# Two graph-attention layers on one core: layer 2's table in degree order, own rows by a plain DMA, another share for TensorE, another seam

## The chip, the cores and the metric

The kernel runs on one core of one Trainium2 chip. The metric is the device time of one execution in microseconds; lower is better. The kernel before takes 5581.57 us, the median of three runs (5579.89 to 5582.52).

## The reference

There are 10000 nodes of 768 features and 170000 edges, sorted by destination (each node has one edge to itself in the list; the layer adds another). All is in fp32. A graph-attention layer projects every node, gives every edge a softmax weight over the edges that end in the same node, and sums the projected source rows with these weights:

```
def gat_conv(x, edge_index, W, a_src, a_dst, bias, heads, out_ch, concat):
    ...
    xl = (x @ W).reshape(n, heads, out_ch)
    alpha_src = jnp.einsum('nhc,hc->nh', xl, a_src)
    alpha_dst = jnp.einsum('nhc,hc->nh', xl, a_dst)
    e = jax.nn.leaky_relu(alpha_src[src] + alpha_dst[dst], 0.2)
    ...                                   # softmax of e over the edges of one dst
    out = jax.ops.segment_sum(xl[src] * alpha[:, :, None], dst, num_segments=n)
    return out + bias

h = gat_conv(x, edge_index, W1, a_src1, a_dst1, b1, 4, 256, True)
h = relu(layer_norm(h, g1, be1)) + (x @ Wr1 + br1)
h1 = h
h = gat_conv(h, edge_index, W2, a_src2, a_dst2, b2, 1, 768, False)
h = layer_norm(h, g2, be2) + (h1 @ Wr2 + br2)
return _layernorm(x + h)
```

## The kernel before

The work has three stages. PE is TensorE, DVE is VectorE, ACT is ScalarE, POOL is GpSimd and SP is SyncE, which only issues DMAs.

**Stage A, the table of layer 1 and the order.** For each of 79 tiles of 128 nodes PE computes x @ W1 (L166, called from L633), ACT and DVE the two attention numbers of every head (L638, L641), and SP stores 128 rows of 1032 floats (4128 B: 1024 features, 4 source and 4 destination numbers) to `table1` (L645). SP also loads x, two tiles ahead (`load_x`, L590). Between the tiles a generator, `prepare` (L185 to L410), does one step at a time of sorting the nodes by their number of in-edges, many first. It computes each node's place in that order (`rank`, L321), scatters node numbers and edge positions to four lists in DRAM (L305), loads these back with SP (`order_d`, L336; 10112 pieces of 16 bytes each), and makes `slots`: for every tile of 128 nodes of nearly equal degree a list of source nodes, one column per slot. Column 0 of a tile is the node itself. A missing edge points to a row of its own at the table's end that weighs nothing. A second generator, `weight_steps`, loads the weights of layer 2 (`w2`) and of layer 1's residual (`wr1`).

**Layer 1** (`ordered_layer1`, L656) goes over the 79 sorted tiles in the order `TURNS`: from few slots (8) up to many (41 in the middle) and down again to 9. The sum over the tiles is 1377 slots. A ring of 28 slots in SBUF (`RING1`) holds gathered rows; `Ring.fetch` issues one indirect DMA on POOL for each slot (`gather`, L413), 128 rows of 4128 B, as soon as the slot's old rows were used. For a tile of n slots `weights_of` takes the softmax weights of all n (`logits`, `normalised`; it needs all n rows) and lets PE sum the first `on_pe(t)` slots (at most `ON_PE1`): ACT makes diagonal matrices of weights (L691) and PE multiplies them with the rows into `acc` (L697). DVE adds the other slots to `acc`: one of `SHARE` = 4 directly with the weight (L496, four instructions), the other three as plain sums (L492) of rows that ACT has multiplied (L485). The weights of the next tile are taken three slots (`LEAD`) before the end of a tile. Then DVE normalises the tile (L538 to L554), adds the residual product x @ Wr1 (L755), PE transposes (L560) and multiplies with W2 (L166, `to_layer2`), SP stores the transposed h1 (L767), ACT copies the product to a row of 770 floats (L716), and POOL scatters this row to `table2` at the nodes' own numbers (`store`, L718), a tile and a half later. POOL also gathers x for the residual (`fetch_x`).

**Layer 2** (`ordered_layer2`, L804) takes the same tiles in the same order with rows of 770 floats (3080 B), one head and a ring of 38 slots (`RING2`). PE sums columns 512 to 767 of every slot (L850, L851), DVE columns 0 to 511 (L496). `residual` computes x + h1 @ Wr2 on PE (L862, L865) from `fetch_x`: h1 loaded by SP (L826), x gathered by POOL. `norms` makes the two layer norms, and POOL scatters the finished rows to the output (L884). At the seam between the layers the first 8 gathers are issued first, then Wr2 is loaded into the space of W2, small vectors are loaded by ACT's queue, and `product(brT, wr2)` gives the constant br1 @ Wr2.

The order within each engine's queue is written out by hand (`manual_schedule`); a queue runs in its order, and waits are on semaphores. The tile of 41 slots does not fit a ring and takes another path (`attend_parts`); no weights are taken ahead for it or for a tile with too many slots after it.

Of the kernel before, what the change touches and what calls it, by code (L numbers as in the profile page):

```python
# [28 lines left out]
F32 = mybir.dt.float32  # L29
# [5 lines left out]
P = 128  # L35
# [10 lines left out]
RING1 = 28  # L46
# [4 lines left out]
SHARE = 4  # L51
ON_PE1 = 5

# [25 lines left out]
def gnn_kernel(ctx, tc, x, x_cols, src, dst, src_col, dst_col, W1, a_src1, a_dst1, b1, g1, be1, Wr1, br1,  # L79
# [5 lines left out]
    C1, C2 = H1 * DH1, H2 * DH2  # L85
    R1, R2 = C1 + 2 * H1, C2 + 2 * H2
    NT = -(-N // P)
# [43 lines left out]
    fits = consts.tile([1, 1], I32, name="fits")  # L131
    lift = consts.tile([P, 1], F32, name="lift")

    def spread(pool, v, name):
# [3 lines left out]
        nc.scalar.dma_start(b, bass.AP(tensor=v.tensor, offset=v.offset, ap=[[0, P], [1, n]]))  # L138
        return b
# [45 lines left out]
    def prepare():  # L185

        with tc.tile_pool(name="prep", bufs=1, side="right") as pool, \
# [146 lines left out]
            with nc.allow_non_contiguous_dma(reason="16 bytes a node"):  # L334
                for to, d in zip([sorted_] + others, order_d):
                    nc.sync.dma_start(to, d.rearrange("(t p) f -> p t f", p=P))  # L336
                    yield
            for other in others:
                nc.vector.tensor_add(sorted_, sorted_, other)
# [89 lines left out]
    class Ring:  # L429


        def __init__(self, pool, table, row, size):
            self.table, self.size, self.issued = table, size, 0
            self.rows = pool.tile([P, size, row], F32, name="ring")

        def fetch(self, upto):
            for q in range(self.issued, min(upto, TOTAL)):
                gather(self.slot(q), self.table[:, :], slots[:, q:q + 1])
                self.issued = q + 1
# [12 lines left out]
    def logits(small, ring, lo, hi, ad, heads, c, top=None):  # L452


        n = hi - lo
        e = small.tile([P, ring.size, heads], F32, name="e")[:, :n]
        for a, b, rows in ring.parts(lo, hi):
            nc.vector.tensor_tensor(e[:, a - lo:b - lo], rows[:, :, c:c + heads],
                                    ad[:, None, :].to_broadcast([P, b - a, heads]), op=OP.add)
# [110 lines left out]
    def spread_br1(pool, name):  # L570

        b = pool.tile([P, K1], F32, name="br1_c")
        with nc.allow_non_contiguous_dma(reason="1024 numbers"):
            nc.scalar.dma_start(b, br1.rearrange("(k p) -> p k", p=P))
        to = pool.tile([P, K1, P], F32, name=name)
        nc.vector.tensor_copy(to, b[:, :, None].to_broadcast([P, K1, P]))
        return to
# [4 lines left out]
    with tc.tile_pool(name="w1", bufs=1) as w1p, tc.tile_pool(name="l1", bufs=2) as io, \  # L582
# [15 lines left out]
        nc.vector.memset(none[:, :C1], 0.0)  # L598
        nc.vector.memset(none[:, C1:], -BIG)
        nc.scalar.dma_start(table1[NP:NP + 1, :], none)  # L600
        nc.scalar.dma_start(table2[NP:NP + 1, :], none[:, C1 - C2:C1 + 2 * H2])
# [5 lines left out]
        def weight_steps():  # L607

            brT = spread_br1(w1p, "brT")
            yield
            yield
            load(w2, W2)
            for i, a in enumerate((a_src2, a_dst2)):
# [16 lines left out]
        for t in range(NT):  # L632
# [23 lines left out]
    def ordered_layer1():  # L656
        nonlocal ps_big
        with tc.tile_pool(name="b1", bufs=1) as pool, tc.tile_pool(name="small1", bufs=2) as small, \
                tc.tile_pool(name="ps_acc1", bufs=2, space=PSUM) as ps_acc, \
                tc.tile_pool(name="ps_h1", bufs=1, space=PSUM) as ps_big, \  # L660
                tc.tile_pool(name="ps_r1", bufs=1, space=PSUM) as ps_r, tc.manual_schedule():
            ring = Ring(pool, table1, R1, RING1)
            ring.fetch(SLOTS[0])
# [10 lines left out]
            def on_pe(t):  # L674


                return min(max((2 * SLOTS[t] - 15) // 5, 1), ON_PE1, SLOTS[t])

            def weights_of(t):

                n, m = SLOTS[t], on_pe(t)
                e, _ = logits(small, ring, FIRST[t], FIRST[t] + n, ring.slot(FIRST[t])[:, C1 + H1:], H1, C1)
                yield e
# [28 lines left out]
            def store(t):  # L712

                nonlocal full
                row = pool.tile([P, R2], F32, name="row")
                nc.scalar.copy(row, full[:, :R2])  # L716
                full = None
                nc.gpsimd.indirect_dma_start(  # L718
                    out=table2[:, :], out_offset=bass.IndirectOffsetOnAxis(ap=nodes(t), axis=0),
                    in_=row, in_offset=None)  # L720

            for t in range(NT + 1):
# [54 lines left out]
                if live and not whole:  # L777
                    due(n)
                    acc = ps_acc.tile([P, 2 * BANK], F32, name="acc")
                    ad = small.tile([P, H1], F32, name="ad")  # L780
                    nc.vector.tensor_copy(ad, ring.slot(FIRST[t])[:, C1 + H1:])
                    attend_parts(small, ring, acc, acc, ad, None, H1, DH1, t)
# [21 lines left out]
    def ordered_layer2():  # L804
        nonlocal ps_big
        with tc.tile_pool(name="b2", bufs=1) as pool, tc.tile_pool(name="small2", bufs=2) as small, \
                tc.tile_pool(name="ps_acc2", bufs=2, space=PSUM) as ps_acc, \
                tc.tile_pool(name="ps_q2", bufs=3, space=PSUM) as ps_big, tc.manual_schedule():
            ring = Ring(pool, table2, R2, RING2)
            ring.fetch(SLOTS[0])  # L810

            wr2, parts = w2[:, :, :C2], [wr1[:, k, :] for k in range(K0)]
            load(wr2, Wr2)
            b2_b, g2_b, be2_b = (spread(pool, v, n) for v, n in ((b2, "b2"), (g2, "g2"), (be2, "be2")))
            more = pool.tile([P, C2], F32, name="out")
            nc.scalar.dma_start(more, bass.AP(tensor=br2.tensor, offset=br2.offset, ap=[[0, P], [1, C2]]))
            nc.vector.tensor_add(be2_b, be2_b, more)
            brT = spread_br1(pool, "brT")
            more = pool.tile([P, C2], F32, name="out")
            nc.scalar.dma_start(more, shift.to_broadcast([P, C2]))  # L820
            nc.vector.tensor_add(b2_b, b2_b, more)

# [114 lines left out]
    def general_path():  # L937
# [82 lines left out]
        def attend_chunks(keep, work, small, lists, table, row, heads, dh, t):  # L1020
# [10 lines left out]
            adm = keep.tile([P, 2 * heads], F32, name="adm")  # L1031
            nc.vector.tensor_copy(adm[:, :heads], acc[:, c + heads:])
            tmp = small.tile([P, heads], F32, name="tmp")
# [172 lines left out]
```

## Time and profile before

| | |
|---|---|
| median of 3 runs | 5581.57 us |
| profiled execution, its own time | 5586.68 us |
| span of its records | 5584.8 us |
| granted TensorE clock, mean | 0.939 |
| busy PE / DVE / ACT / POOL | 4822.9 / 4279.6 / 3140.8 / 3367.2 us |
| moved by DMA | 1581 MB, mean 283 GB/s |
| gathers of rows (L413) | 2754, 954 ns each |
| scatters of layer 2's rows (L718) | 79, 1079 ns each |
| stage A, layer 1, layer 2 | about 0 to 890, 890 to 3530, 3540 to 5585 us |

The profile is that of one execution. Busy is time in which an engine runs an instruction; issuing a DMA by SP is not counted, while POOL's indirect DMAs are[...]. In the timeline and the waits, what stands after an arrow is the event that ended an idle time. A busy PE is modelled and not PE at its peak. Landing of a DMA is counted from its issue.

### The profile page before, as it was taken

What the parts mean: (1) busy time and instruction counts of PE and PEld (TensorE: products, weight loads), DVE (VectorE), ACT (ScalarE), POOL (GpSimd) and SP (SyncE); (2) the same over time, 40 slices, a digit from 0 to 9 for tenths busy, and PEclk for the clock granted to TensorE, in tenths of its full rate; (3) what the DMA queues carried; (4) which work ended last, traced back from release to release, by engine and by line L of the source; (5) the groups of instructions that cost most, each with busy time, mean ns of one, the idle gap of its engine ahead of it and who ended that gap; (6) DMA issues with size and microseconds to landing.
All of it is one profiled execution on the core that took longest, in us unless ns stands there. A gap on an engine that the chain in (4) does not pass through costs nothing. (4 is left out here: it accounts for less than half of the span.)

```text
span 5584.8 us, 58282 instructions
## 1 busy us (share of the span) xinstructions
PE 4822.9 (86%) x15304; PEld 2875.9 (51%) x15304; DVE 4279.6 (77%) x7692; ACT 3140.8 (56%) x8177; POOL 3367.2 (60%) x3396
## 2 busy tenths in 40 slices
PE   9999997999998874678899999799988737888988
PEld 3444443555555542345555555466555525555555
DVE  5783344888988778777899888498877776778888
ACT  3433444788888776677888887243333312334333
POOL 2446465555655554455566553477777776777775
PEclk9999998999999997789999999899998878999999
DMA  4322426899998887788999986699999987999996
GB/s 156 123 93 81 100 90 258 304 324 334 338 348 331 312 306 289 276 306 323 339 356 346 343 319 238 244 339 340 332 332 330 331 290 261 332 327 328 336 335 235
DMA packets 438663, 1581.00 MB, mean 283 GB/s; under 512 B 102763, under 2 KB 106923, under 8 KB 438326
## 3 DMA queue, kind: packets, MB, share of 16 engines
q0 software_dynamic: 341344, 1400.80, 69.9%
q1 hardware_dynamic: 93168, 170.98, 9.1%
q10 hardware_dynamic: 3814, 5.39, 0.3%
q8 instruction: 129, 2.11, 0.1%
q14 instruction: 208, 1.70, 0.1%
HBM read 1431.10 MB, written 146.19 MB: 282 GB/s over the span
## 5 line engine op out<-in xcount | busy, mean ns | idle before, releaser
L413 POOL DMA_INDIRECT ring<-table,slots x2754 | 2626.3, 954 | 1361.8 <-issue 290.4
L496 DVE SCALAR_TENSOR_TENSOR acc<-ring,e,acc 128x256 f32<-128x256 f32 (+1 forms) x2486 | 1546.5, 622 | 193.0 <-PE acc L697 119.4
L485 ACT ACTIVATE ring<-ring,e 128x256 f32<-128x256 f32 x3236 | 1317.2, 505 | 0.0
L492 DVE TENSOR_TENSOR acc<-acc,ring 128x1024 f32<-128x1024 f32 x809 | 996.6, 1232 | 71.2 <-ACT ring L485 2.1
L865 PE MATMUL big<-w,wr 128*128 128x512 f32 (+1 forms) x2528 | 877.4, 501 | 0.0
L166 PE MATMUL big<-w,xT 128*128 128x512 f32 x1896 | 823.7, 596 | 19.8 <-DMA w<-in_W_dram 9.4
L166 PE MATMUL big<-w,hT 128*128 128x512 f32 (+1 forms) x2528 | 830.4, 486 | 1.2 <-ACT hT L563 1.2
L166 PE MATMUL big<-wr,xT 128*128 128x512 f32 x1896 | 830.4, 595 | 0.7 <-ACT xT L563 0.7
L851 PE MATMUL big<-ring,diagonals 128*128 128x256 f32 x2672 | 646.6, 403 | 153.0 <-ACT diagonals L850 121.5
L697 PE MATMUL acc<-ring,diagonals 128*128 128x256 f32 x2088 | 516.6, 407 | 265.9 <-ACT diagonals L691 265.8
L865 PEld LDWEIGHTS big<-w,wr 128*128 128x128 f32 x2528 | 494.4, 196 | 369.6 <-issue 335.8
L166 PEld LDWEIGHTS big<-w,hT 128*128 128x128 f32 x2528 | 478.3, 189 | 373.5 <-issue 340.7
L851 PEld LDWEIGHTS big<-ring,diagonals 128*128 128x128 f32 x2672 | 533.5, 202 | 262.5 <-ACT diagonals L850 168.1
L166 PEld LDWEIGHTS big<-w,xT 128*128 128x128 f32 x1896 | 361.8, 192 | 479.2 <-issue 460.7
L697 PEld LDWEIGHTS acc<-ring,diagonals 128*128 128x128 f32 x2088 | 424.4, 206 | 351.0 <-ACT diagonals L691 253.2
L166 PEld LDWEIGHTS big<-wr,xT 128*128 128x128 f32 x1896 | 356.1, 191 | 418.5 <-issue 417.4
L850 ACT ACTIVATE diagonals<-ident,e 128x128 f32<-128x128 f32 x1336 | 398.6, 387 | 152.8 <-DVE e L476 113.5
L542 ACT ACTIVATE sd<-mv,eps 128x1 f32<-128x1 f32 x237 | 69.8, 294 | 592.8 <-DVE mv L540 592.3
L638 DVE TENSOR_TENSOR scr<-big,as_b 128x1024 f32<-128x1024 f32 x79 | 96.7, 1225 | 382.0 <-ACT row L635 382.0
L691 ACT ACTIVATE diagonals<-ident,e 128x128 f32<-128x128 f32 x1044 | 318.9, 387 | 110.8 <-DVE e L476 110.8
L643 POOL TENSOR_TENSOR row<-row,none 128x1024 f32<-128x1024 f32 x79 | 186.9, 2366 | 270.4 <-ACT row L635 269.9
L466 ACT ACT_TABLE_LOAD x153 | 196.3, 1283 | 238.8 <-DVE e L465 210.2
(169 smaller groups left out, 3971.4 us busy)
## 6 DMA issues: line engine op xcount, KB each, us to landing
ring<-table,slots POOLq DMA_INDIRECT x2754, 6.0
table<-row SPq DMA_DIRECT2D x79, 516.0 KB, 2.9
h_d<-hT SPq DMA_DIRECT2D x79, 512.0 KB, 7.2
wr<-h_d SPq DMA_DIRECT2D x79, 512.0 KB, 6.9
xT<-in_x_cols_dram SPq DMA_DIRECT2D x79, 384.0 KB, 4.4
w<-in_W_dram SPq DMA_DIRECT2D x6, 512.0 KB, 7.3
w<-in_W_dram SPq DMA_DIRECT2D x1, 3072.0 KB, 13.4
wr<-in_Wr_dram SPq DMA_DIRECT2D x1, 3072.0 KB
```

Source lines behind the costliest of these rows:

```text
L166: nc.tensor.matmul(p[:, c:e], aT[:, j, :], w[:, j, c:e], start=(j == 0), stop=(j == k - 1))
L413: nc.gpsimd.indirect_dma_start(out=to, out_offset=None, in_=table, in_offset=bass.IndirectOffsetOnAxis(ap=index, axis=0), **more)
L466: nc.scalar.activation(e, e, AF.Exp)
L485: nc.scalar.activation(row[:, s], row[:, s], AF.Copy, scale=e[:, h:h + 1])
L492: nc.vector.tensor_add(acc[:, :c], acc[:, :c], row[:, :c])
L496: nc.vector.scalar_tensor_tensor(acc[:, s], row[:, s], e[:, h:h + 1], (acc if first is None else first)[:, s], op0=OP.mult, op1=OP.add)
L643: nc.gpsimd.tensor_add(row[:, :C1], row[:, :C1], b1_b)
L691: nc.scalar.activation(diagonals[:, k * H1 + i, :], ident, AF.Copy, scale=e[:, k, i:i + 1])
L697: nc.tensor.matmul(acc[:, c:d], diagonals[:, k * H1 + i, :], ring.slot(FIRST[t] + k)[:, c:d], start=(k == 0 and c % BANK == 0), stop=(k == ...
L850: nc.scalar.activation(diagonals[:, k % G, :], ident, AF.Copy, scale=e[:, k, :])
L851: nc.tensor.matmul(to, diagonals[:, k % G, :], ring.slot(FIRST[t] + k)[:, ON_PE2:C2], start=False, stop=(k == n - 1), skip_group_check=True)
L865: nc.tensor.matmul(r[:, c:d], hT[:, j, :], wr2[:, j, c:d], start=False, stop=(j == K1 - 1 and (d < C2 or not whole(t))), skip_group_check= ...
```

## The change

Layer 2's table is now indexed by rank, the place in the sorted order, and not by node number.

1. `prepare` writes the ranks with one more SP DMA as a last column of `table1` (10112 pieces of 4 bytes); the rows grow to 1033 floats (4132 B). The stores of stage A leave the column out.
2. In layer 1 the gathered rows bring their nodes' ranks. After Exp, `logits` copies the rank column of the tile's slots over `slots` (ACT, as int32), so that layer 2 gathers by rank.
3. `store` writes the 128 rows of a tile to consecutive rows of `table2`, by a plain DMA of SP in place of POOL's scatter.
4. In layer 2 the first slot of each tile, the nodes' own rows, is loaded by a plain DMA of SP in place of a gather (`own`).
5. `ON_PE1` is 4 in place of 5, and `on_pe` has another formula. Over the tiles PE's slots go from 261 to 227: one less in tiles of 13, of 15, and of 20 to 27 slots; DVE and ACT take these.
6. Seam: br1 is loaded once in stage A. Wr2 goes to the space of Wr1. Wr2 and the five small vectors are loaded by SP ahead of the first gathers. `product(brT, wr2)` and `residual(1)` come after PE's share of tile 0.

```diff
-ON_PE1 = 5
+ON_PE1 = 4
...
-    R1, R2 = C1 + 2 * H1, C2 + 2 * H2
+    R1, R2 = C1 + 2 * H1 + 1, C2 + 2 * H2
...
+                nc.sync.dma_start(table1[:NP, R1 - 1:].rearrange("(p j) r -> p (j r)", p=P), rank)
+                yield
...
         def fetch(self, upto):
             for q in range(self.issued, min(upto, TOTAL)):
-                gather(self.slot(q), self.table[:, :], slots[:, q:q + 1])
+                if q in self.own:
+                    nc.sync.dma_start(self.slot(q), self.table[self.own[q] * P:(self.own[q] + 1) * P, :])
+                else:
+                    gather(self.slot(q), self.table[:, :], slots[:, q:q + 1])
                 self.issued = q + 1
...
         nc.scalar.activation(e, e, AF.Exp)
+        if not ring.own:
+            for a, b, rows in ring.parts(lo, hi):
+                nc.scalar.copy(slots[:, a:b], rows[:, :, R1 - 1])
         return e, new
...
-            nc.sync.dma_start(table1[t * P:(t + 1) * P, :], row)
+            nc.sync.dma_start(table1[t * P:(t + 1) * P, :R1 - 1], row[:, :R1 - 1])
...
-            ring = Ring(pool, table1, R1, RING1)
+            ring = Ring(pool, table1, R1, RING1, {})
...
-                return min(max((2 * SLOTS[t] - 15) // 5, 1), ON_PE1, SLOTS[t])
+                return min(max(SLOTS[t] // 2 - 5, 1), ON_PE1, SLOTS[t])
...
-                nc.gpsimd.indirect_dma_start(
-                    out=table2[:, :], out_offset=bass.IndirectOffsetOnAxis(ap=nodes(t), axis=0),
-                    in_=row, in_offset=None)
+                nc.sync.dma_start(table2[TURNS[t] * P:(TURNS[t] + 1) * P, :], row)
...
-            ring = Ring(pool, table2, R2, RING2)
-            ring.fetch(SLOTS[0])
-
-            wr2, parts = w2[:, :, :C2], [wr1[:, k, :] for k in range(K0)]
-            load(wr2, Wr2)
-            b2_b, g2_b, be2_b = (spread(pool, v, n) for v, n in ((b2, "b2"), (g2, "g2"), (be2, "be2")))
...
+            wr2 = wr1.rearrange("p k n -> p (k n)")[:, :K1 * C2].rearrange("p (k n) -> p k n", n=C2)
+            load(wr2, Wr2)
+            parts = pieces(w2.rearrange("p k n -> p (k n)")[:, :6 * C1], C1)
+            b2_b, g2_b, be2_b = (spread(pool, v, n, nc.sync)
+                                 for v, n in ((b2, "b2"), (g2, "g2"), (be2, "be2")))
+            adds = [spread(pool, br2, "out", nc.sync), spread(pool, shift, "brT", nc.sync)]
+            ring = Ring(pool, table2, R2, RING2, dict(zip(FIRST, TURNS)))
+            ring.fetch(SLOTS[0])
+            nc.vector.tensor_add(be2_b, be2_b, adds[0])
+            nc.vector.tensor_add(b2_b, b2_b, adds[1][:, :C2])
             brT = spread_br1(pool, "brT")
...
-            q = product(brT, wr2, C2)
...
-                if t + 1 < NT:
+                if 0 < t < NT - 1:
                     rs[t + 1] = residual(t + 1)
...
                     acc = ps_acc.tile([P, BANK], F32, name="acc")
+                    if not t:
+                        q = product(brT, wr2, C2)
+                        rs[1] = residual(1)
                     next(last, None)
```

More of the change, by code (lines that the diff above doesn't have):

```diff
@@ L132, in gnn_kernel, with spread @@
     lift = consts.tile([P, 1], F32, name="lift")
-    def spread(pool, v, name):
+    br1_c = consts.tile([P, K1], F32, name="br1_c")
+    def spread(pool, v, name, queue=None):
         n = v.shape[-1] if len(v.shape) == 1 else v.shape[0] * v.shape[1]
         b = pool.tile([P, n], F32, name=name)
-        nc.scalar.dma_start(b, bass.AP(tensor=v.tensor, offset=v.offset, ap=[[0, P], [1, n]]))
+        (queue or nc.scalar).dma_start(b, bass.AP(tensor=v.tensor, offset=v.offset, ap=[[0, P], [1, n]]))
         return b
@@ L429, in gnn_kernel, with __init__ @@
     class Ring:
-        def __init__(self, pool, table, row, size):
-            self.table, self.size, self.issued = table, size, 0
+        def __init__(self, pool, table, row, size, own):
+            self.table, self.size, self.own, self.issued = table, size, own, 0
             self.rows = pool.tile([P, size, row], F32, name="ring")
@@ L570, in spread_br1 @@
     def spread_br1(pool, name):
-        b = pool.tile([P, K1], F32, name="br1_c")
-        with nc.allow_non_contiguous_dma(reason="1024 numbers"):
-            nc.scalar.dma_start(b, br1.rearrange("(k p) -> p k", p=P))
         to = pool.tile([P, K1, P], F32, name=name)
-        nc.vector.tensor_copy(to, b[:, :, None].to_broadcast([P, K1, P]))
+        nc.vector.tensor_copy(to, br1_c[:, :, None].to_broadcast([P, K1, P]))
         return to
@@ L599, in gnn_kernel @@
         nc.vector.memset(none[:, C1:], -BIG)
+        nc.vector.memset(none[:, R1 - 1:], float(NP))
         nc.scalar.dma_start(table1[NP:NP + 1, :], none)
@@ L607, in weight_steps @@
         def weight_steps():
-            brT = spread_br1(w1p, "brT")
+            with nc.allow_non_contiguous_dma(reason="1024 numbers"):
+                nc.scalar.dma_start(br1_c, br1.rearrange("(k p) -> p k", p=P))
             yield
             yield
+            brT = spread_br1(w1p, "brT")
             load(w2, W2)
@@ L674, in on_pe @@
             def on_pe(t):
-                return min(max((2 * SLOTS[t] - 15) // 5, 1), ON_PE1, SLOTS[t])
+                return min(max(SLOTS[t] // 2 - 5, 1), ON_PE1, SLOTS[t])
             def weights_of(t):
                 n, m = SLOTS[t], on_pe(t)
-                e, _ = logits(small, ring, FIRST[t], FIRST[t] + n, ring.slot(FIRST[t])[:, C1 + H1:], H1, C1)
+                e, _ = logits(small, ring, FIRST[t], FIRST[t] + n, ring.slot(FIRST[t])[:, C1 + H1:C1 + 2 * H1], H1, C1)
                 yield e
@@ L780, in ordered_layer1 @@
                     ad = small.tile([P, H1], F32, name="ad")
-                    nc.vector.tensor_copy(ad, ring.slot(FIRST[t])[:, C1 + H1:])
+                    nc.vector.tensor_copy(ad, ring.slot(FIRST[t])[:, C1 + H1:C1 + 2 * H1])
                     attend_parts(small, ring, acc, acc, ad, None, H1, DH1, t)
@@ L808, in ordered_layer2 @@
                 tc.tile_pool(name="ps_q2", bufs=3, space=PSUM) as ps_big, tc.manual_schedule():
-            ring = Ring(pool, table2, R2, RING2)
-            ring.fetch(SLOTS[0])
-            wr2, parts = w2[:, :, :C2], [wr1[:, k, :] for k in range(K0)]
-            load(wr2, Wr2)
-            b2_b, g2_b, be2_b = (spread(pool, v, n) for v, n in ((b2, "b2"), (g2, "g2"), (be2, "be2")))
-            more = pool.tile([P, C2], F32, name="out")
-            nc.scalar.dma_start(more, bass.AP(tensor=br2.tensor, offset=br2.offset, ap=[[0, P], [1, C2]]))
-            nc.vector.tensor_add(be2_b, be2_b, more)
+            wr2 = wr1.rearrange("p k n -> p (k n)")[:, :K1 * C2].rearrange("p (k n) -> p k n", n=C2)
[5 more added lines that the diff above has]
+            ring = Ring(pool, table2, R2, RING2, dict(zip(FIRST, TURNS)))
+            ring.fetch(SLOTS[0])
+            nc.vector.tensor_add(be2_b, be2_b, adds[0])
+            nc.vector.tensor_add(b2_b, b2_b, adds[1][:, :C2])
             brT = spread_br1(pool, "brT")
-            more = pool.tile([P, C2], F32, name="out")
-            nc.scalar.dma_start(more, shift.to_broadcast([P, C2]))
-            nc.vector.tensor_add(b2_b, b2_b, more)
             def fetch_x(t):
@@ L1031, in attend_chunks @@
             adm = keep.tile([P, 2 * heads], F32, name="adm")
-            nc.vector.tensor_copy(adm[:, :heads], acc[:, c + heads:])
+            nc.vector.tensor_copy(adm[:, :heads], acc[:, c + heads:c + 2 * heads])
             tmp = small.tile([P, heads], F32, name="tmp")
```

## The prediction

> **What bounds the kernel now.** I read the busy time in stretches first (stage A, the table, ends near 890 us; layer 1 runs to about 3530; layer 2 to the end), then the waits in a stretch of each layer, then the timeline of one tile and of the seam. Columns of the stretches: length, busy time of PE, PEld, DVE, ACT and POOL with instruction counts, granted clock, share of the DMA engines in use, GB/s.
>
> ```profile
> core 0: us, PE busy (x) PEld busy (x) DVE busy (x) ACT busy (x) POOL busy (x), PEclk, DMA share, GB/s
> ...
> 2400.00:2800.00 400.00, 342.94 (x1150) 215.29 (x1151) 318.53 (x478) 317.48 (x795) 226.51 (x242) 0.94 0.87 320
> 2800.00:3200.00 400.00, 382.17 (x1303) 230.63 (x1302) 362.64 (x572) 339.78 (x829) 242.84 (x256) 1.00 0.94 351
> ...
> 3600.00:4000.00 400.00, 376.77 (x1316) 247.33 (x1315) 346.09 (x751) 167.83 (x395) 303.86 (x316) 0.98 0.94 335
> 4000.00:4400.00 400.00, 337.87 (x1137) 227.73 (x1136) 317.42 (x645) 151.65 (x381) 303.88 (x316) 0.90 0.94 331
> 4400.00:4800.00 400.00, 247.79 (x835) 170.37 (x834) 287.74 (x535) 106.88 (x279) 280.11 (x284) 0.80 0.85 293
> 4800.00:5200.00 400.00, 337.62 (x1131) 225.53 (x1130) 322.09 (x656) 151.29 (x373) 303.73 (x315) 0.92 0.93 329
> ```
>
> In layer 2, POOL's 304 of 400 us looks like slack and is not. The waits of 3600 to 4400 show why:
>
> ```profile
> DVE e L458 <- DMA ring<-table,slots: 80.6, 21, 6.6
> ...
> POOL ring L413 <- issue: 47.8, 157, 0.3
> ...
> POOL ring L413 <- PE big L851: 36.1, 99, 6.3
> ```
>
> Nearly every pause of POOL is 0.3 us (47.8 over 157; the PE pauses hold the one of 6.3). So an indirect DMA costs 0.95 + 0.30 = 1.25 us, and 316 of them are 395 of 400 us: POOL issues without rest, while DVE waits for rows. The bursts of layer 1, with larger rows, have the same 1.25 us, so it is a cost of issuing and not of the transfer. **Layer 2 is bound by POOL**, except around 4510 to 4640 (the tile of 41 slots) and in the tail. The DMA engines are next: 0.94 in use.
>
> In layer 1 POOL does 256 operations, 320 of 400 us. Its waits (2300 to 3400):
>
> ```profile
> POOL ring L413 <- DVE acc L492: 105.9, 152, 8.0
> ...
> POOL table L718 <- ACT row L716: 72.9, 33, 3.9
> ...
> DVE acc L496 <- PE acc L697: 45.7, 26, 3.9
> ...
> DVE e L458 <- DMA ring<-table,slots: 39.0, 13, 6.6
> ```
>
> POOL stands 73 us behind the store of layer 2's row, which waits for ACT, with gathers queued behind it. A tile of 22 slots shows what follows:
>
> ```profile
> 1986.10 1.01 POOL L718 DMA_INDIRECT table<-row,order  x1 [3.91 <-ACT row L716]
> 1987.41 0.96 POOL L413 DMA_INDIRECT ring<-table,slots  x1 [0.30 <-PE acc L697]
> ...
> 1988.72 2.06 DVE L496 SCALAR_TENSOR_TENSOR acc<-ring,e,acc 128x256 f32<-128x256 f32 x4 [3.30 <-PE acc L697]
> ...
> 2015.45 0.25 DVE L458 TENSOR_TENSOR e<-ring 128x92 f32<-128x92 f32 x1 [5.00 <-DMA ring<-table,slots]
> ```
>
> Gathers start after the store, run back to back, and the last row that the next logits need lands 28 us later; DVE waits 5.00 for it. From one L716 copy to the next is 25.1 us at 12 slots, 26.9 at 14, 28.8 at 16, 31.0 at 18, 33.2 at 19, 36.3 at 20, 38.8 at 21, 42.4 at 22, 45 to 53 above. Up to 16 the steps follow PE's share; from 18 the bytes decide (18 rows of 528 KB and 1.3 MB besides take 30.6 us at 353 GB/s), plus waits.
>
> **What the Trainium skill says.** All in "DMA: Bandwidth & Descriptors". *Issuing engines are not separate DMA queues*: issuing from several engines saves only sequencer time, usually small. Here that time is the limit of layer 2, so moving an issue to SP counts. *SWDGE vs HWDGE vs iDMA*: GpSimd computes its descriptors in software, SP's are made by hardware; the trace agrees, 1.25 us of POOL against 0.3 to 0.4 of SP for a store. *Where 436 GB/s comes from*: about 358 GB/s of HBM for a core; the best slices here, 356 and 351, agree. *How a descriptor splits into AXI transactions*: a read starts at the 256 B boundary below it; used below for the longer row.
>
> **Part by part**, against the profiled execution (5586.7 us, span 5584.8, some 5 above the median).
>
> *Layer 2's own rows by SP.* 79 gathers leave POOL: 79 x 1.25 = 99 us of the bound. SP only loads h1 there and spends 1956 us waiting for PE; the own load of tile t+3 stands behind the h1 load of t+2, which waits for a product of tile t, finished a tile earlier, so I cost that at nothing. About 4 of the 79 fall in the stalled middle, and the lightest 10 tiles are nearly as much DVE's: DVE is 346 + gaps of 400 in the first stretch. That leaves some 85. The bytes stay: 646 MB. At the old pace they need 335 GB/s; 85 us less of some 1990 asks for 347, close to the 351 that layer 1 sustained at the same share of 0.94. So part turns into DMA wait: I take 70, bounds 30 (rows held near 340 GB/s) and 99.
>
> *Layer 2's row stored by SP.* In layer 1 79 x 1.3 us leave POOL, and the wait for L716. By itself POOL is no limit, but in the 22-slot tile the first two gathers wait only for PE's first two slots, which end some 5 us before the store does; then the burst starts 4 to 5 us earlier and the 5.00 mostly goes. Limit: the bytes (353 GB/s give 33.7 us at 20, 36.7 at 22, 39.6 at 24). So: 6 tiles of 20 by 2, 4 of 21 by 3, 4 of 22 by 4, seven larger by 4.3 on average: 12 + 12 + 16 + 30 = 70. Tiles of 18 and 19 lose 0.4 and 0.9: 9. On SP the store stands ahead of the h1 store, whose input comes 7 us later anyway: nothing.
>
> *Share for TensorE.* 261 slots become 227. By the timeline each takes 1.8 us from PE (16 matmul records of two slots in 3.62), 1.23 from ACT's diagonals (8 in 2.45), and gives DVE 1.29 (21 slots, with 1.65 of ACT) or 2.06 (13 slots). Tiles of 13 and 15 go from PE's bound to DVE's (24.55 + 2.06 busy + 1.7 of gaps and waits = 28.3 at 15, against 28.25 now): about nothing, bounds +15 and -20. From 20 slots up PE's wait of 3.30 shrinks by some 2, which the 70 contains, and DVE's extra slot lies under the transfer.
>
> *Ranks.* ACT copies one column per tile, 125 pieces after Exp. The nearest row is Exp itself at 0.24 us: 30 us of ACT, under the 1.4 us that ACT waits there for DVE's weights (L691 <- DVE e L476, 47.7 us over 34 tiles). Nothing; bounds 0 and +15. The row grows to 4132 B: 0.1% of bytes, and by the page's rule about one beat of 133 for starts no longer on 32 B; an estimate of 0.8% on tiles bound by bytes, some 1000 us: +8. The rank write has 10112 pieces, like the loads of order_d (8.7 us to land, PE full in that stretch), and x is loaded two tiles (20 us) ahead: nothing, up to +10. One memset and one small load more or less: nothing, under stage A's PE.
>
> *Seam.*
>
> ```profile
> 3531.67 0.97 POOL L718 DMA_INDIRECT table<-row,order  x1 [12.88 <-ACT row L716]
> ...
> 3540.01 0.98 POOL L413 DMA_INDIRECT ring<-table,slots  x1 [7.38 <-DMA table<-row,order]
> ...
> 3599.37 0.94 POOL L413 DMA_INDIRECT ring<-table,slots  x1 [6.26 <-PE big L851]
> ```
>
> The last store goes ahead of the 3 MB of Wr2 on one queue and lands in about 2.9 us (stage A's stores): gathers start near 3535.5, 4.5 earlier. Tile 0's share precedes the product with brT (10.5 us) and residual(1), so the 6.26 goes. Wr2 still waits behind the store: no gain from its new place. Sum 11, bounds 0 and 25 (5 MB ahead of the first own row on SP are 15 us, under the x gathers; DVE's wait for br_c, 14.0, goes too, but PE's residual(0) ends as late).
>
> **Sum:** 70 + 70 + 9 + 11 - 8 = 152 less: 5586.7 - 152 = 5435, less 5 for the median: **5430**.
>
> **Rivals.** (1) Layer 2 only: layer 1 keeps its waits, because ring slots, not the store, hold the gathers (105.9 us wait for DVE's freeing; the landing that follows speaks against). 70 + 11 - 8: about 5508. (2) Layer 2 gives little: the engines at 0.94 are full and 335 GB/s is the limit of 3080 B rows. Then 30 there and 82 elsewhere: about 5470. Against it, a slice of layer 2 shows 344 GB/s. (3) Slower: the 4132 B row. Gathers are one packet of 4128 B, 160 ns at the median, 181 mean in the packet records. If an odd length costs an extra piece or partial write, the 764 slots of tiles from 18 up bear it: 8 packets per engine each, so 25 ns per packet (14%) eats the whole 152 us, and 40 ns (244 us) gives 5430 + 244 = 5675. A smallest packet takes 9 ns, which costs 55 us and leaves a gain; rows of 3080 B, no multiple of 32, run at the same 26 B per ns. (4) No effect, the own loads on SP arriving late: 1.9 us per tile would cancel it; SP is idle, so little.
>
> **Numbers.** Forecast 0.62, rival 1 0.16, rival 2 0.14, rival 3 0.05, no effect 0.03. A measurement tells 0.2% (11 us) from no change. Faster 0.92, same 0.03, slower 0.05. The range reaches from full relief in layer 2 and 100 in layer 1 (about 5375) to rival 1 with its own spread: 5370 to 5525.
>
> **What would show it.** POOL in 4000 to 4400 still near 1.25 us per operation, 79 fewer in all, DMA share 0.96 or more and over 342 GB/s; L458's wait for rows shorter in layer 1, L718 gone from POOL; tiles of 22 at 38 to 39 us; the first gather of layer 2 within 5 us of the last L716 copy. Wrong if the L413 packets of layer 1 got longer, if POOL idles on slots in layer 2, or if tiles of 13 and 15 grew by over 1 us.

## The result, and the profile after

The changed kernel takes **5483.16 us** (median of 4 runs, 5481.5 to 5488.77), the kernel before 5582.05 us on the same chip: ratio 0.9825, interval 0.9808 to 0.9842. That is 99 us less. The forecast was 5430, and 5483 lies in its range of 5370 to 5525. The profiled execution took 5488.77 us, its span 5487.0.

The starts of each tile's row copy (layer 1, now L728) and output activation (layer 2, now L891) in the two traces give the account. Each number is the change of a stage's length, after minus before:

| stage | forecast | measured |
|---|---|---|
| stage A, up to the first row copy of layer 1 | 0 (up to +10) | +12.7 |
| layer 1 | -71 (-79 for the store, +8 for the longer row) | -60.4 |
| seam, up to the first output of layer 2 | -11 | -13.8 |
| layer 2, up to its last output | -70 | -40.8 |
| tail | 0 | +4.5 |
| sum (span) | -152 | -97.8 |

Layer 1 and the seam held in sign and roughly in size. Layer 2 gave a bit over half, and stage A lost a little more than the upper bound that I had left.

The stretches of the kernel after (columns as in the prediction):

```profile
core 0: us, PE busy (x) PEld busy (x) DVE busy (x) ACT busy (x) POOL busy (x), PEclk, DMA share, GB/s
...
2400.00:2800.00 400.00, 351.84 (x1166) 215.31 (x1165) 351.34 (x535) 337.47 (x847) 236.60 (x243) 0.95 0.94 346
2800.00:3200.00 400.00, 378.77 (x1275) 224.75 (x1274) 365.50 (x571) 336.50 (x831) 234.64 (x241) 1.00 0.96 345
...
3550.00:3950.00 400.00, 389.31 (x1380) 258.89 (x1379) 356.37 (x772) 173.54 (x413) 297.78 (x309) 0.99 0.96 347
3950.00:4350.00 400.00, 332.75 (x1119) 229.09 (x1117) 312.05 (x633) 146.00 (x363) 288.93 (x300) 0.90 0.93 329
4350.00:4750.00 400.00, 248.80 (x848) 173.60 (x849) 292.47 (x545) 114.42 (x301) 273.53 (x276) 0.80 0.86 295
4750.00:5150.00 400.00, 347.47 (x1169) 233.22 (x1168) 331.19 (x680) 155.49 (x386) 292.95 (x306) 0.92 0.94 339
```

Before, POOL did 316 operations in 400 us of layer 2 outside the stretch with the tile of 41 slots. Now it does 309, then 300. So **POOL is no longer the limit in the second stretch**, and yet the bytes move no faster there: 329 GB/s, before 331. The waits of 3600 to 4400 say what POOL does instead (columns: total us, times, longest). First a line of the kernel before:

```profile
POOL ring L413 <- DVE acc L496: 22.2, 73, 0.3
```

Then the kernel after:

```profile
DVE e L467 <- DMA ring<-table,slots: 79.9, 20, 8.1
...
POOL ring L418 <- issue: 48.5, 148, 1.5
POOL ring L418 <- DVE acc L508: 39.6, 83, 2.8
POOL ring L418 <- PE big L860: 39.2, 122, 1.5
```

Look at the longest ones. Before, no wait of POOL for a slot that DVE frees was longer than 0.3 us in this window. Now they last up to 2.8 us. All of POOL's pauses over 0.45 us between layer 2's first and last gather come to 106 us, in 53 pieces; before they were 44 us in 9 pieces. By tiles: the gain lies in the light tiles at both ends (10 us in the first twenty, of up to 17 slots, and 30 us in the last twenty-seven, of up to 19), and the thirty-two tiles of 17 to 41 slots between them gained 1 us together.

In layer 1 the scatter is gone from POOL (waits of 2300 to 3400; first a line of the kernel before):

```profile
POOL ring L413 <- DVE acc L496: 82.1, 100, 2.9
```

```profile
POOL ring L418 <- DVE acc L508: 151.9, 125, 2.8
POOL ring L418 <- DVE acc L504: 150.0, 259, 5.7
...
DVE e L467 <- DMA ring<-table,slots: 8.1, 8, 2.6
```

The wait of the next logits for rows fell from 39.0 to 8.1 us in this stretch, as the forecast said. What took its place is POOL waiting for DVE's freeing: 302 us at DVE's two additions (L508 and L504), against 188 before (82.1 at L496 and 105.9 at L492). A tile of 22 slots shows how:

```profile
1969.52 0.78 ACT L728 COPY row<-big 128x770 f32<-128x770 f32 x1
1970.33 0.32 SPq L730 DMA_DIRECT2D table<-row  x1
1970.84 0.94 POOL L418 DMA_INDIRECT ring<-table,slots  x1 [0.30 <-PE acc L709]
...
1981.33 0.93 POOL L418 DMA_INDIRECT ring<-table,slots  x1 [1.17 <-DVE acc L508]
1982.67 0.93 POOL L418 DMA_INDIRECT ring<-table,slots  x1 [0.41 <-DVE acc L504]
1984.01 0.93 POOL L418 DMA_INDIRECT ring<-table,slots  x1 [0.41 <-DVE acc L504]
1985.34 0.93 POOL L418 DMA_INDIRECT ring<-table,slots  x1 [0.41 <-DVE acc L504]
1987.44 0.93 POOL L418 DMA_INDIRECT ring<-table,slots  x1 [1.17 <-DVE acc L508]
...
1999.62 0.25 DVE L467 TENSOR_TENSOR e<-ring 128x92 f32<-128x92 f32 x1 [3.66 <-DMA ring<-table,slots]
...
2011.15 0.78 ACT L728 COPY row<-big 128x770 f32<-128x770 f32 x1
```

The store is 0.32 us of SP and nobody waits for it. The burst runs, but no longer back to back: four gathers take 6.11 us (1981.33 to 1987.44), 1.53 each instead of 1.25, because each waits for the slot that DVE just used. This tile takes 41.6 us from copy to copy, 43.1 before; the four of 22 slots take 40.4 on average, against 42.4 before and the 38 to 39 of the forecast.

The seam, where the last row goes to the table and the first gather of layer 2 reads it:

```profile
3482.95 0.80 ACT L728 COPY row<-big 128x770 f32<-128x770 f32 x1 [12.44 <-PE big L169]
3483.77 0.32 SPq L730 DMA_DIRECT2D table<-row  x1
...
3487.87 0.95 POOL L418 DMA_INDIRECT ring<-table,slots  x1 [87.96 <-issue]
```

The first gather starts 4.1 us after the store is issued, and 4.9 after the start of the copy (within 5 was the forecast).

And stage A, SP's queue: the load of x behind the last load of `order_d` in the kernel before, then the same place and the write of the ranks in the kernel after:

```profile
642.08 6.10 SPq L590 DMA_DIRECT2D xT<-in_x_cols_dram  x1
```

```profile
644.61 6.83 SPq L599 DMA_DIRECT2D xT<-in_x_cols_dram  x1
654.01 0.32 SPq L657 DMA_DIRECT2D table<-row  x1
654.43 0.61 SPq L341 DMA_DIRECT2D table<-rank  x1
655.13 13.07 SPq L599 DMA_DIRECT2D xT<-in_x_cols_dram  x1
...
668.77 0.38 SPq L599 DMA_DIRECT2D xT<-in_x_cols_dram  x1
```

The rank DMA itself is issued in 0.61 us. The load of x behind it, a 0.38 us affair otherwise, takes 13.07 us to issue, and the loads of x then come too late: of 20 us from 660 on, PE works 12.91. In this part of stage A the tiles follow each other by 10.3 us; here there are 20.6 us between two of them, so the write costs 10.3 us in this trace.

```profile
PE big L169 <- DMA xT<-in_x_cols_dram: 7.1, 1, 7.1
```

### The profile page after: what moved, and what is told of

It reads as the page before. It is cut to its first block, busy times and chain, and to the rows that moved or that the text cites. A ratio compares the mean times of both kernels' runs of the same rounds, so it can differ in the third digit from the quotient of the medians.

```text
span 5487.0 us, 58297 instructions
## 1 busy us (share of the span) xinstructions
PE 4754.0 (87%) x15032; PEld 2827.1 (52%) x15032; DVE 4328.8 (79%) x7766; ACT 3148.0 (57%) x8255; POOL 3247.4 (59%) x3238
## 5 line engine op out<-in xcount | busy, mean ns | idle before, releaser
L418 POOL DMA_INDIRECT ring<-table,slots x2675 | 2591.7, 969 | 1635.6 <-DVE acc L508 402.4
L508 DVE SCALAR_TENSOR_TENSOR acc<-ring,e,acc 128x256 f32<-128x256 f32 (+1 forms) x2538 | 1572.0, 619 | 127.5 <-PE acc L709 52.0
L497 ACT ACTIVATE ring<-ring,e 128x256 f32<-128x256 f32 x3320 | 1351.0, 505 | 0.0
L504 DVE TENSOR_TENSOR acc<-acc,ring 128x1024 f32<-128x1024 f32 x830 | 1022.5, 1232 | 72.8 <-ACT ring L497 1.2
L874 PE MATMUL big<-wr,w 128*128 128x512 f32 (+1 forms) x2528 | 857.9, 493 | 0.0
L860 PE MATMUL big<-ring,diagonals 128*128 128x256 f32 x2672 | 660.8, 409 | 185.3 <-ACT diagonals L859 177.0
L709 PE MATMUL acc<-ring,diagonals 128*128 128x256 f32 x1816 | 456.6, 409 | 247.9 <-ACT diagonals L703 216.5
L874 PEld LDWEIGHTS big<-wr,w 128*128 128x128 f32 x2528 | 488.1, 193 | 350.3 <-issue 317.7
L709 PEld LDWEIGHTS acc<-ring,diagonals 128*128 128x128 f32 x1816 | 370.1, 206 | 326.8 <-ACT diagonals L703 235.7
L859 ACT ACTIVATE diagonals<-ident,e 128x128 f32<-128x128 f32 x1336 | 399.6, 387 | 155.6 <-DVE e L488 117.9
L703 ACT ACTIVATE diagonals<-ident,e 128x128 f32<-128x128 f32 x908 | 278.5, 387 | 96.4 <-DVE e L488 96.4
```

What stands on the lines that cost most here:

```text
L418: nc.gpsimd.indirect_dma_start(out=to, out_offset=None, in_=table, in_offset=bass.IndirectOffsetOnAxis(ap=index, axis=0), **more)
L497: nc.scalar.activation(row[:, s], row[:, s], AF.Copy, scale=e[:, h:h + 1])
L504: nc.vector.tensor_add(acc[:, :c], acc[:, :c], row[:, :c])
L508: nc.vector.scalar_tensor_tensor(acc[:, s], row[:, s], e[:, h:h + 1], (acc if first is None else first)[:, s], op0=OP.mult, op1=OP.add)
L703: nc.scalar.activation(diagonals[:, k * H1 + i, :], ident, AF.Copy, scale=e[:, k, i:i + 1])
L709: nc.tensor.matmul(acc[:, c:d], diagonals[:, k * H1 + i, :], ring.slot(FIRST[t] + k)[:, c:d], start=(k == 0 and c % BANK == 0), stop=(k == ...
```

## Experiments

My theory at this point: own rows and store are the gain, as forecast; layer 2's middle is held by something behind POOL. The rivals for that something were the transfers (bytes), the depth of the ring, and a loop of waits through the ring. The first eight experiments ran on chips where layer 2 moves its rows more slowly and the kernel before takes 6036 to 6039 us (the kernel after 5829), so they are compared with each other and by ratio; the last four ran where before takes 5582 to 5585. On the slower chips the change is worth more (0.9657 of before, against 0.9825), and POOL is not the limit of layer 2 there even with the layer 2 of the kernel before (before_share_new, described below, whose layer 2 is unchanged: 261 operations in 400 us, not 316):

```profile
4000.00:4400.00 400.00, 310.70 (x951) 203.80 (x951) 260.24 (x537) 129.88 (x310) 247.75 (x261) 0.84 0.81 274
```

So what an undone part costs there tells in which layer it acts; the size does not carry over to the chip of the first comparison. "Issue stretch" is the time from a layer's first to its last gather into the ring.

**own_by_pool.** Part of the change undone: in `fetch` the own rows are gathered by POOL again.

```diff
-                if q in self.own:
-                    nc.sync.dma_start(self.slot(q), self.table[self.own[q] * P:(self.own[q] + 1) * P, :])
-                else:
-                    gather(self.slot(q), self.table[:, :], slots[:, q:q + 1])
+                gather(self.slot(q), self.table[:, :], slots[:, q:q + 1])
```

> The changed kernel with one part undone: in layer 2 the own rows are gathered by POOL again, by rank. If POOL's issue were the whole limit of layer 2, as the forecast had it, 79 x 1.25 us come back: 70 to 99 us more than the changed kernel's 5483, so 5553 to 5580. If layer 2 in the changed kernel is limited by something else from about 18 slots up (the ring of 38 slots, or the DMA engines), as its trace suggests (layer 2 shrank by only 40), it is 35 to 45 us: about 5523. In both cases layer 1 stays as in the changed kernel.

**store_by_pool.** The store scatters from POOL again, to ranks.

```diff
-                nc.sync.dma_start(table2[TURNS[t] * P:(TURNS[t] + 1) * P, :], row)
+                nc.gpsimd.indirect_dma_start(
+                    out=table2[:, :],
+                    out_offset=bass.IndirectOffsetOnAxis(ap=slots[:, FIRST[t]:FIRST[t] + 1], axis=0),
+                    in_=row, in_offset=None)
```

> The changed kernel with one part undone: layer 2's rows are scattered by POOL again, to the ranks. Forecast's theory: the scatter holds the gathers up in tiles of 18 slots and more, so nearly all of layer 1's gain of 62 us goes: 5483 + 55 = about 5540, with the loss in tiles of 18 to 27 slots. Rival: slots of the ring hold the gathers anyway and the share for TensorE brought the gain: at most 15 us more, 5485 to 5498. The seam loses some 4 us in both.

**share_old** gives the kernel after the share of before; **before_share_new** gives the kernel before the new share alone:

```diff
-ON_PE1 = 5
+ON_PE1 = 4
...
-                return min(max((2 * SLOTS[t] - 15) // 5, 1), ON_PE1, SLOTS[t])
+                return min(max(SLOTS[t] // 2 - 5, 1), ON_PE1, SLOTS[t])
```

> The changed kernel with the old share for TensorE (at most 5, 261 slots). Forecast's theory: tiles of 13 and 15 cost PE's time again but nothing on the whole (by the traces 13 gained 1.3 us each, 15 about 0.1: +7), and tiles from 20 up wait some 1 to 2 us longer for PE: together 10 to 40 us more, 5493 to 5523. Rival (share brought layer 1's gain): 45 or more, 5528 and up.

> The kernel before with the new share alone. If the shares act by themselves, 10 to 40 us less than 5582: 5542 to 5572. If they only help once the store has left POOL (the gathers of the freed slots still stand behind it), within 10 us of before. If DVE's extra slots bind, slower.

Measured, these four on one chip (before 6036.25):

| kernel | us | ratio to before, interval | issue stretch layer 1 / layer 2 |
|---|---|---|---|
| own_by_pool | 5917.44 | 0.9797, 0.9779 to 0.9816 | 2511.8 / 2361.7 |
| store_by_pool | 5914.43 | 0.9802, 0.9786 to 0.9818 | 2587.3 / 2268.9 |
| share_old | 5834.99 | 0.9672, 0.9655 to 0.9690 | 2511.2 / 2266.3 |
| before_share_new | 6008.13 | 0.9951, 0.9934 to 0.9967 | 2596.4 / 2374.0 |

Each edit acts in its own layer. With the scatter back on POOL, layer 1's stretch is 76 us longer and layer 2's is the same; its old wait is back too (waits of store_by_pool, 2300 to 3400):

```profile
POOL table L730 <- ACT row L728: 50.8, 26, 2.7
```

With the own rows back on POOL, layer 2's stretch is 94 us longer (2361.7 against 2268.9 and 2266.3) and layer 1's is the same. 94 over 79 gathers is 1.19 us each. That is the size I expected if POOL's issue were the whole limit, but POOL has slack on this chip (own_by_pool):

```profile
4000.00:4400.00 400.00, 315.73 (x968) 206.82 (x968) 267.25 (x546) 129.97 (x316) 249.69 (x262) 0.84 0.81 273
```

262 operations in 400 us are 1.53 us each. So the run shows that the own rows by SP help layer 2, but not that it is POOL's issue time that they save: the gather's own transfer, which a plain load replaces, or its place in the loop below would do as well, and no run takes these apart. The two undone parts together (94 and 76 us) are already more than the 99 us that the whole change gave on the first chip. The share is worth 28 us on the kernel before, for which the forecast had no term of its own. On the kernel after, where I expected the old share to cost 10 to 40 us, it costs no more than the spread: the ratios 0.9672 and 0.9657 (after_again below, on another such chip) have overlapping intervals. The relief of DVE and PE by the store and by the share overlaps; the share alone is not to be added to the rest.

**after_again, no_own, ring41, rank_split**, on a second such chip (before 6038.51). The first is the kernel after, unchanged. no_own leaves out the own rows' loads beyond the first 38 slots of layer 2 (5% of its bytes):

```diff
                 if q in self.own:
-                    nc.sync.dma_start(self.slot(q), self.table[self.own[q] * P:(self.own[q] + 1) * P, :])
+                    if q < self.size:
+                        nc.sync.dma_start(self.slot(q), self.table[self.own[q] * P:(self.own[q] + 1) * P, :])
```

ring41 has three more slots:

```diff
-RING2 = 38
+RING2 = 41
```

rank_split writes the rank column in ten parts of at most 1024 pieces, one with each step of the loop that writes `order_d`, so also earlier than the loads of `order_d`:

```diff
+                if sent < NT:
+                    with nc.allow_non_contiguous_dma(reason="4 bytes a node"):
+                        nc.sync.dma_start(ranks[:, sent:upto], rank[:, sent:upto])
+                sent = upto
...
-                nc.sync.dma_start(table1[:NP, R1 - 1:].rearrange("(p j) r -> p (j r)", p=P), rank)
```

> The changed kernel itself, beside the three others on the same chip, since the first four runs came from a chip on which the kernel before takes 6036 us and layer 2 moves 270 to 290 GB/s. On a chip like the first: 0.9825 of before (5483). On the slow chip, from the stage times of the first four runs (layer 1 as in share_old, layer 2 likewise), 0.966 to 0.970 of before.

> The changed kernel without the loads of layer 2's own rows, but for the first 38 slots (later tiles read what the slot held before). It leaves out 31 MB of 646 MB of layer 2. If the DMA engines or the memory limit layer 2 after the change, layer 2 shrinks by up to 4.8%, 60 to 90 us less than the changed kernel. If POOL's issue or the depth of the ring limits it, nothing of the POOL's work changes: 0 to 20 us less.

> The changed kernel with a ring of 41 slots in layer 2 in place of 38 (the tile of 41 slots then fits). If the ring's depth limits tiles from 18 slots up, POOL's pauses of 1 to 3 us per tile go and the big tile takes the quick path: 25 to 60 us less than the changed kernel. If the DMA engines limit layer 2: within 10 us, but for some 10 to 20 us of the big tile.

> The changed kernel with the rank column written by ten DMAs of at most 1024 pieces, one to a step, in place of one of 10112 pieces. The trace of the changed kernel shows the x load behind the one DMA issuing for 13 us and PE out of x for 7 us, and the tiles of stage A 10 us late after it. If the one DMA is the cause, stage A is 9 to 11 us shorter. If writes of 4 bytes as such disturb the stores and loads beside them, the ten cost as much: 0 to 4 us.

| kernel | us | ratio to before, interval |
|---|---|---|
| after_again | 5828.82 | 0.9657, 0.9629 to 0.9684 |
| no_own | 5833.96 | 0.9659, 0.9631 to 0.9686 |
| ring41 | 5836.15 | 0.9665, 0.9638 to 0.9692 |
| rank_split | 5822.29 | 0.9643, 0.9619 to 0.9666 |

5% of the bytes less: nothing. Three slots more: nothing, not even the 10 to 20 us that I expected in any case of the tile of 41 slots. I took this first for a sign against a limit by ring slots; the code shows why it need not be one. `turn`, the place in a tile where DVE takes the next tile's logits, is computed from `ring.size`: in tiles from 20 slots up, three more slots put it two or three slots earlier. The gathers run further ahead, and DVE asks for them earlier by nearly as much. In rank_split the stall of stage A is gone. One of the ten parts, and then SP's queue at the time of the stall above:

```profile
589.13 0.39 SPq L337 DMA_DIRECT2D table<-rank  x1
589.60 0.96 SPq L604 DMA_DIRECT2D xT<-in_x_cols_dram  x1
...
650.93 0.38 SPq L604 DMA_DIRECT2D xT<-in_x_cols_dram  x1
...
661.24 0.37 SPq L604 DMA_DIRECT2D xT<-in_x_cols_dram  x1
```

Behind a part, the load of x takes about 1 us to issue. The copies of stage A (L652, L647 in the kernel after) never stand more than 10.3 us apart from 500 us on, where after_again has one gap of 20.7. Of all fourteen traces, the nine with the one rank DMA have such a gap at that place (15.8 to 20.8 us), and the five without it or with the parts have none. So the one DMA costs 5.5 to 10.5 us. Whether the size of the parts or their earlier place removes it was not taken apart. In the medians, 5822 against 5829, the intervals overlap.

**turn_later, half_rows, best.** From here on the theory was the loop. DVE frees a slot, POOL gathers into it, the row lands, the next logits need that row, and while DVE waits for it DVE frees nothing. The trace of the kernel after, a tile of 20 slots:

```profile
4162.14 1.54 DVE L508 SCALAR_TENSOR_TENSOR acc<-ring,e,acc 128x512 f32<-128x512 f32 x2
...
4168.60 0.21 DVE L467 TENSOR_TENSOR e<-ring,ad 128x20 f32<-128x20 f32 x1 [4.81 <-DMA ring<-table,slots]
...
4170.85 0.94 POOL L418 DMA_INDIRECT ring<-table,slots  x1 [1.31 <-issue]
```

DVE stands 4.81 us for a row, and then POOL has a pause of 1.31 where it had 0.30. turn_later puts the logits four slots later, that is, gives the row 3 us more (by the formula in tiles of 19 slots and more; two slots at 18, one at 17, none below):

```diff
-                        turn = min(max(n // 3, n + SLOTS[t + 1] + 2 * LEAD - ring.size), n - LEAD)
+                        turn = min(max(n // 3, n + SLOTS[t + 1] + 2 * LEAD + 4 - ring.size), n - LEAD)
```

> The kernel after, with one number changed: in layer 2 the logits of the next tile are asked for four slots later within a tile (DVE weighs four more rows, 3 us, before it waits for the next tile's last row). Theory: since the change, layer 2's middle (tiles of 18 to 27 slots) is set by a loop through the ring: DVE frees a slot, POOL gathers into it, the row lands 6.5 us later, and DVE waits for it at the next logits (wait of L467 for ring rows, 66 us in 600 on the first chip) while it frees nothing, so that POOL pauses. Then the later place takes 20 to 40 us away: 5790 to 5810 where the kernel after takes 5829, ratio about 0.962. Rival 1, the transfers themselves are the limit: nothing, 5829 within 8. Rival 2, TensorE's share, which starts after the logits, is pushed back and frees slots later: slower, 5840 to 5860.

half_rows leaves the place of the logits as it is and leaves out the first half of each gathered row (half of the bytes):

```diff
+                half = R2 // 2
...
+                    nc.sync.dma_start(self.slot(q)[:, half:], self.table[self.own[q] * P:(self.own[q] + 1) * P, half:])
...
+                    gather(self.slot(q)[:, half:], self.table.rearrange("n (two r) -> (n two) r", two=2),
+                           slots[:, q:q + 1])
```

> The kernel after, with layer 2's gathers and own-row loads bringing only the second half of each row (1540 B in place of 3080 B; the first half of the ring is set to zero once): part of the computation is left out, all instructions of POOL, DVE, PE and ACT stay. Theory 1, a loop of latency and issue: layer 2's issue stretch (2258 us) falls only a little, to 2150 to 2250, and POOL goes on pausing on slots. Theory 2, the transfers (bytes, or the time of a packet in a slow engine): it falls by 300 us or more, until POOL is the limit again, at some 1535 operations without the own rows = 1450 by 1.25 = 1810 us. In both the setting to zero costs up to 15 us at the seam.

> The kernel after with the rank column written in ten pieces (as in rank_split), a ring of 41 rows in layer 2 and the next tile's logits four slots later. If the loop of slots and landings limits layer 2's middle, the larger ring now pays as well, since the logits stay where they are and gathers run three slots further ahead: 20 to 50 us below rank_split's 5822, ratio 0.956 to 0.961. If the transfers limit it: as rank_split, 0.964.

These ran where before takes 5582.13 us, so the numbers beside them are those of the first comparison (after 5483.16, 0.9825, layer 2's stretch 1937.9):

| kernel | us | ratio to before, interval | issue stretch layer 2 |
|---|---|---|---|
| turn_later | 5442.24 | 0.9754, 0.9739 to 0.9769 | 1903.0 |
| half_rows | 5427.05 | 0.9723, 0.9705 to 0.9741 | 1894.1 |
| best | 5420.23 | 0.9715, 0.9701 to 0.9728 | 1877.3 |

turn_later is 41 us faster than the kernel after, at the upper end of what I expected of the loop. Its layer 2 is shorter in the trace by 35 us of the stretch, and by 32 from the first output to the last. The rest lies ahead of layer 2, where the edit changes nothing, and is spread between executions; I count 35 for the edit. The thirty-two tiles of 17 to 41 slots, to which the change had given nothing, gain 40 us; the tiles behind them lose 9. POOL's pauses over 0.45 us fall from 106 to 65 us, and POOL is the limit again (stretches of turn_later):

```profile
3550.00:3950.00 400.00, 389.31 (x1383) 259.51 (x1382) 354.25 (x765) 175.15 (x418) 299.97 (x311) 0.99 0.97 349
3950.00:4350.00 400.00, 337.37 (x1144) 231.52 (x1142) 328.61 (x662) 148.62 (x371) 303.12 (x316) 0.91 0.95 346
```

316 operations instead of 300 in the second stretch, 346 GB/s instead of 329: **the same transfers that were taken to be near their limit run 5% faster once they are asked for later**. What DVE stood idle ahead of the logits L467 for rows of the ring, in the whole of layer 2 (3500 to 5450), in the kernel after:

```profile
DMA ring<-table,slots: 171.8, 45
```

and a fifth less in turn_later:

```profile
DMA ring<-table,slots: 138.7, 46
```

half_rows shows how much the bytes could hold at most (its stretches):

```profile
3550.00:3950.00 400.00, 389.90 (x1390) 260.21 (x1389) 354.97 (x766) 177.74 (x419) 299.71 (x310) 0.99 0.70 207
3950.00:4350.00 400.00, 339.45 (x1155) 232.66 (x1154) 329.93 (x665) 150.09 (x376) 303.74 (x317) 0.92 0.68 199
```

With 0.68 of the DMA engines in use and 199 GB/s, POOL does its 317 operations and is the limit. What I expected of each theory was worked out for a stretch of 2258 us and can't be held against one of 1938: here POOL's own time (1449 operations at 1.28 us in this trace, 1860 us, and nine longer pauses of 38 us together) is the whole stretch and ends the fall before it tells the two apart. Together with turn_later it does tell. Halving the bytes takes 44 us off the stretch; 35 can be had with every byte in place, from asking four slots later. So for no more than some 9 us are the bytes needed as a cause. Rows of half the size land in 3.3 us at the median in place of 5.8: a shorter landing and a later question help alike, as they should if both are legs of one loop.

best takes turn_later, ring41 and rank_split together (the logits then stand one slot later than in the kernel after: four later by the edit, three earlier by the ring), and beats both kernels: 5420.23 us, 162 us below before and 63 below after. Against turn_later, layer 2's stretch is 26 us shorter. By the starts of the outputs, 15 of these lie around the tile of 41 slots, which fits a ring of 41. No run on this chip has the larger ring alone.

**before_turn_later.** If the loop became a limit only through the change, the same edit does nothing to the kernel before.

> The kernel before, with only the one number of turn_later: layer 2's next logits four slots later. Theory: the wait of the next logits for the last row became a limit of layer 2 only through the change; before it, POOL issued 316 operations in 400 us without a pause in the same tiles, so nothing is to be had: 5582 within 11, ratio 0.998 to 1.002. Rival: the later place is worth the same anywhere (38 to 44 us, as on the kernel after): 5540 to 5545, ratio 0.993.

Measured: 5584.04 us against 5584.55, ratio 1.0001, interval 0.9992 to 1.0010. In its trace POOL's counts are those of before:

```profile
3600.00:4000.00 400.00, 378.14 (x1308) 246.28 (x1307) 347.49 (x758) 168.64 (x396) 303.36 (x317) 0.97 0.94 336
4000.00:4400.00 400.00, 337.21 (x1147) 228.87 (x1146) 320.64 (x650) 151.37 (x381) 303.71 (x317) 0.91 0.94 332
```

An edit worth 35 us on the kernel after is worth nothing on the kernel before: before, DVE waited at the same place, but for a POOL that hardly paused. That settles it for the chips where these four ran. Open is how much of layer 2's middle is the same loop on the chips where before takes 6036 us: turn_later wasn't run there. no_own shows only that 5% of the bytes don't matter there.

## Why the prediction was right or wrong

- **The number**: 5483 lies in the range, but so do rivals 1 (5508) and 2 (5470). It is the stages and the runs that speak for the mechanism, not the total. Of the forecast's own signs, the scatter left POOL, the wait of layer 1's logits got shorter and the first gather of layer 2 came within 5 us. But one of its signs of being wrong came too: POOL waits for slots in layer 2, and the DMA share there is 0.93 at 329 GB/s, not 0.96 and over 342.
- **POOL as the bound of layer 2**: right on the chips where before takes 5582 to 5585. Before, POOL issued 316 operations in 400 us with hardly a pause, and asking for the rows later changed nothing (before_turn_later). With 79 gathers fewer and the later question it issues 316 again. own_by_pool (94 us) does not show it, since it ran where POOL is not the limit.
- **What layer 2 gives**: the mechanism was right, the term mis-sized: 70 forecast, 40.8 measured, inside its bounds of 30 and 99. The step that failed is "So part turns into DMA wait". I looked for the next limit only among the engines' shares, took the DMA engines at 0.94 for it, and cut 85 to 70. Their limit was further off: turn_later and best reached 345 to 352 GB/s. (The rate that I asked of them was also a little low: 335 GB/s times 1990 over 1905 is 350, not 347.) Nearer was a limit that is no engine's: the loop of slot, gather, landing and logits. The line that I quoted for POOL's bound, DVE's 80.6 us for rows, belongs to this loop. In the kernel before it was POOL's effect, as I read it. What I did not ask is what DVE's waiting would hold up once POOL was faster: the wait is as long after the change (79.9 us), and now POOL pauses behind it. With turn_later added, layer 2 gives 72.6 by the same measure. That is near the 70, but it takes another edit.
- **Store by SP**: right in kind. Undoing it brings the wait for ACT back and costs 76 us of layer 1's stretch on the slower chip. On the first chip layer 1 gave 60.4 in all, and by tiles it fell short where it was to be largest: tiles of 22 gained 2.0 where I had put 4, the larger ones 0.2 to 2.7 where I had put 4.3. The step that failed is "then the burst starts 4 to 5 us earlier": I let it keep its 1.25 us per gather. In fact it runs at DVE's pace, 1.53. That is the mechanism of rival 1, ring slots holding the gathers, and it took part of the gain but not all. The five tiles of 13 slots, from which I expected nothing, gave 1.3 us each; whether the store or the share did that was not taken apart.
- **Share**: no term of its own; PE's shorter wait from 20 slots up was counted inside the 70 of the store. On top of the rest the share is worth nothing beyond share_old's spread; alone on the kernel before it is 28 us, where the old scatter still held the bursts. Both were measured on the slower chip.
- **Ranks**: the step "x is loaded two tiles (20 us) ahead: nothing, up to +10" failed. I counted the landing of the rank DMA and not what stands behind it on SP: the next issue takes 13 us. The kernel before showed the sign, 6.10 us behind a load of `order_d`. The cost is 10.3 us in the profiled trace.
- **The 4132 B row**: packets of layer 1's gathers take 183.4 ns on average against 180.9 before, 1.4% (0.8% forecast), at the median 161 against 160. No extra piece; rival 3 is out.
- **Seam**: 13.8 against 11.
- **Rival 2** came nearest in time, for another reason than its own: it had the transfers full at 335 GB/s. **Rival 4**, the own loads arriving late, is out: in the profile after, one wait of 1.5 us in layer 2 ended with such a load.

## What to carry to other kernels

When an engine that bounds a stage is relieved, the next limit need not be an engine: follow one buffer slot round (freed, refilled, landed, asked for) and count how much work lies between asking and need. A consumer that waits in order for the newest row holds back the slots which the next rows need. Asking a few slots later gave 35 us here once POOL was relieved, and nothing before that. And when a ring is made deeper, look whether the place of the question moves with it: it did in ring41, and depth alone changed nothing there.

## What was not expected of the hardware

A DMA of 10112 pieces of 4 bytes is issued by SP in 0.61 us, and the next DMA on SP then takes 13.07 us to issue, one behind the loads of `order_d` 6.83, against 0.38 otherwise. Behind a part of at most 1024 such pieces, written earlier and with a step of other work between, it takes 0.96. On the slower chips 79 gathers moved from POOL to SP are worth 94 us, 1.19 us each, though POOL does only 261 operations in 400 us there; which part of a gather costs this stays open.
